# Inverse-times-value and score-times-f products of a delta-rule layer on four 64x64 TensorE tiles, with the second key head's f crossed between the partition halves

## The chip, the cores and the metric

The kernel runs on one core of a Trainium2 chip. The metric is the device time of one execution in microseconds, the median of several runs. Each core has a matrix engine (PE, TensorE; its weight loads are shown as PEld), a vector engine (DVE), a scalar engine (ACT), a general engine (POOL, GpSimd) and a queue engine that issues DMAs (SP). Each of them works through its own instructions in order and waits for the others by semaphores.

## The reference, cut to what matters

The program is two transformer layers on an input of 2 batches x 1024 tokens x 256. Layer 0 adds a gated delta-rule attention and a mixture of low-rank experts; layer 1 adds a gated linear attention and a sparsified feed-forward unit. The change lies in the delta-rule layer, which takes most of the time. It has 16 key heads of 128 and 32 value heads of 128; two value heads share a key head. After projections, a causal convolution over four tokens and SiLU, each value head runs this recurrence over its tokens:

```
S = S * exp(g_t)                      # state, 128 x 128
kv = k_t @ S
delta = (v_t - kv) * beta_t
S = S + outer(k_t, delta)
o_t = q_t @ S
```

with q and k normalized, g and beta from a second projection. The outputs are multiplied by SiLU(z), normalized by their root mean square, scaled, and projected by W_out.

## The kernel before

All is in float32, for which each matrix product is issued as two instructions.

**Tiling.** The 128 partitions hold both batches side by side: a chunk is 64 tokens of batch 0 in the lower half (LO) and the same 64 tokens of batch 1 in the upper half (HI). A head group is 4 value heads and their 2 key heads (8 groups); a unit is one group and 512 columns, that is 4 chunks (4 units to a group); a pair is two chunks. There are 64 pairs and 128 chunks. The recurrence is done chunk by chunk, with the inverse of a unit triangular 64x64 matrix for each head and batch.

**Steps of a pair.** `pair_scores` (L489) multiplies keys by keys and queries into the PSUM tile kq (PE, L520), and by the decays lb on DVE (L526) into np: np[:, 0] for the inverse, np[:, 1] for the outputs. SP then copies np[:, 0] in two ways: four DMAs into nat (L530), and two DMAs to DRAM (natd, L536), from where eight small DMAs (L540) gather n, the 8x8 diagonal blocks. `pair_lanes` inverts these on DVE in a chain of small operations on X (L558 to L582) and sends the result E through DRAM (ed, L584) into U (L586). `pair_inverse` joins blocks to 32 with two rounds of 32x32 products (L603), then to 64 (px L660, xs L663, pyt L669), and leaves the transposed inverses in invT, where they are copied by L654 and L671. invT is a 128x128 block diagonal for each head: batch 0's inverse at LO x LO, batch 1's at HI x HI, zeros elsewhere, set once.

**Steps of a chunk.** `chunk_tokens` (L675) turns keys and values to tokens by partitions: ktok on POOL (L688), vtok on ACT (L697). `chunk_state` multiplies the old state by keys (pks) and queries (pqs, both L716), subtracts pks from vtok on DVE (L719), scales the state on POOL (L724), forms pf = invT x vtok (L734), copies it to f on ACT (L736), multiplies keys with f into pS (L743) and scores with f into po (L747), adds pS to the state on DVE (L754), po to qs (L758), multiplies by z (L760), and squares on ACT (gsq, L765). `chunk_output` computes the root mean square on POOL (ms and rms, L775 to L779), scales z (L782), turns it (yT, L786, copied to yTs on ACT, L788) and projects it (out, L792); DVE adds that to the result (L794).

pf is four products over all 128 partitions, one for each head. pS works on 64x64 tiles: from each half of the partitions to both halves of a PSUM tile, one bank for each batch. po works on two 64x64 tiles only: LO to LO and HI to HI, in one bank.

**Order.** The loop over pairs of `delta_layer` (L835) has steps of several pairs in flight: the scores and lanes of pair p, the inverse of p - 1, states of p - 2, the last outputs of p - 3, and convolutions of later units. `in_windows` (L817) merges them by due times, and a scheduler places each engine's instructions; the order is fixed when the program is built. The first chunk of a pair is called even here, the second odd.

**Buffers.** PSUM has 8 banks in one rotating pool of 512-column tiles, all under one tag, for the whole program. Work tiles have two buffers unless another number is given.

```
add("scores", 0.0, 0.45, pair_scores(k, pools, pair(p)))
add("lanes", 0.65, 0.9, pair_lanes(k, pools, pair(p)), "scores")
add("inverse", 0.0, 1.0, pair_inverse(k, pools, pair(p - 1)))
add("tokens0", 0.5, 1.0, chunk_tokens(k, pools, pair(p - 1).chunks[0]), "state0")
add("tokens1", 0.0, 0.4, chunk_tokens(k, pools, two))
add("state0", 0.0, 0.5, chunk_state(k, pools, one))
add("state1", 0.5, 1.0, chunk_state(k, pools, two), "state0", "tokens1")
```

Of the kernel before, what the change touches and what calls it, by code (L numbers as in the profile page):

```python
# [9 lines left out]
F32 = mybir.dt.float32  # L10
# [4 lines left out]
P = 128  # L15
D = 256
KT = D // P
NB = 2
# [161 lines left out]
def delta_gates(k, pool, I):  # L180


    nc = k.nc
    shape = [P, NTILE, HV]
    wba = pool.tile([P, KT, 2 * HV], F32, tag="wba", name="wba")
    nc.sync.dma_start(wba, I["W_ba"].rearrange("(kt p) c -> p kt c", p=P))
    dtb = pool.tile([P, HV], F32, tag="dtb", name="dtb")
    nc.scalar.dma_start(dtb, I["dt_bias"].partition_broadcast(P))
    na = pool.tile([P, HV], F32, tag="na", name="na")
    nc.scalar.dma_start(na, I["A_log"].partition_broadcast(P))  # L190

    nbeta = k.gates.tile(shape, F32, tag="nbeta", name="nbeta")
    g = pool.tile(shape, F32, tag="g", name="g")
    x = pool.tile(shape, F32, tag="spx", name="spx")
    for t, rows in thin_projection(k, pool, "ba", wba, 2 * HV):
        pv = rows.rearrange("p t (m c) -> p t m c", m=HK)
        mine = lambda a: a[:, t : t + TPB, :].rearrange("p t (m c) -> p t m c", m=HK)
        nc.scalar.activation(mine(nbeta), pv[:, :, :, 0:2], AF.Sigmoid)
        nc.vector.tensor_copy(mine(x), pv[:, :, :, 2:4])
        yield  # L200
    nc.vector.tensor_scalar(nbeta, nbeta, -1.0, None, ALU.mult)
    yield
    nc.vector.tensor_tensor(x, x, bcast(dtb, 1, NTILE), ALU.add)
    yield

    u = pool.tile(shape, F32, tag="spu", name="spu")
    nc.scalar.activation(u, x, AF.Abs)
    nc.scalar.activation(u, u, AF.Exp, scale=-1.0)  # L210
    s = pool.tile(shape, F32, tag="sps", name="sps")
    nc.vector.tensor_scalar(s, u, 2.0, None, ALU.add)
    yield
    nc.vector.reciprocal(s, s)
    yield
    nc.vector.tensor_tensor(s, s, u, ALU.mult)
    yield
    s2 = pool.tile(shape, F32, tag="sps2", name="sps2")
    nc.vector.tensor_tensor(s2, s, s, ALU.mult)
    yield  # L220
    nc.vector.tensor_scalar(u, s2, 1.0 / 17.0, None, ALU.mult)
    yield
    for d in (15, 13, 11, 9, 7, 5, 3):
        nc.vector.scalar_tensor_tensor(u, u, 1.0 / d, s2, ALU.add, ALU.mult)
        yield
    nc.vector.scalar_tensor_tensor(u, u, 1.0, s, ALU.add, ALU.mult)
    yield
    nc.vector.tensor_scalar(x, x, 0.0, None, ALU.max)
    yield
    nc.vector.scalar_tensor_tensor(x, u, 2.0, x, ALU.mult, ALU.add)  # L230
    yield
    nc.scalar.activation(na, na, AF.Exp)
    nc.vector.tensor_scalar(na, na, -1.0, None, ALU.mult)
    yield
    nc.vector.tensor_tensor(g, x, bcast(na, 1, NTILE), ALU.mult)
    yield

    flat = lambda a: a.rearrange("p t h -> p (t h)")
    sums = {}
    for name, lhsT in (("neG", k.upto), ("nrev", k.after)):  # L240
        ps = ps_tile(k, f"sum_{name}")
        nc.tensor.matmul(ps, lhsT, flat(g), start=True, stop=True)
        sums[name] = k.gates.tile(shape, F32, tag=name, name=name)
        nc.scalar.activation(flat(sums[name]), ps, AF.Exp)
        yield
    k.eEnd = k.gates.tile([P, NB, NTILE, HV], F32, tag="eEnd", name="eEnd")
    for b, rows in enumerate((LO, HI)):
        ps = ps_tile(k, f"sum_end{b}")
        nc.tensor.matmul(ps, k.ones[rows], flat(g)[rows], start=True, stop=True)
        nc.scalar.activation(flat(k.eEnd[:, b]), ps, AF.Exp)  # L250
        yield
    for name in ("neG", "nrev"):
        nc.vector.tensor_scalar(sums[name], sums[name], -1.0, None, ALU.mult)


    gT = pool.tile([HV, NTILE, P], F32, tag="gT", name="gT")
    for t0 in range(0, NTILE, 4):
        ps = ps_tile(k, f"gT{t0}")
        for i in range(4):
            nc.tensor.transpose(ps[0:HV, i * P : (i + 1) * P], g[:, t0 + i, :], k.ident)  # L260
        nc.scalar.copy(gT[:, t0 : t0 + 4, :].rearrange("h t c -> h (t c)"), ps[0:HV, :])
        yield
    k.grows = k.dram.tile([NGROUP, NB, NTILE, HPG, CT], F32, tag="grows", name="grows")
    for b in range(NB):
        mine = gT[:, :, b * CT : (b + 1) * CT]
        nc.vector.memset(mine[:, :, 0:1], -1e30)
        for n in range(NGROUP):
            nc.sync.dma_start(k.grows[n, b].rearrange("t h c -> h t c"), mine[n * HPG : (n + 1) * HPG])
    k.nbeta = nbeta
    k.neG, k.nrev = sums["neG"], sums["nrev"]  # L270
# [218 lines left out]
def pair_scores(k, pools, pr):  # L489
# [6 lines left out]

    nc, wk, h = k.nc, pools.work, pr.h
    pr.nat = wk.tile([P, PC, HPG, B], F32, tag="nat32", name=f"nat32{pr.name}")  # L500
    pr.n8 = wk.tile([P, W, W], F32, tag="n8", name=f"n8{pr.name}")
# [19 lines left out]
    yield  # L521
    pr.np = pools.np.tile([P, 2, PC, HPG, CT], F32, tag="np", name=f"np{pr.name}")
    pairs = lambda a: a.rearrange("p x (m j) i -> p (x m) j i", m=KPG)
    for s in range(2):
        by = kq[:, :, :, s].rearrange("p x m i -> p (x m) i")
        nc.vector.tensor_tensor(pairs(pr.np[:, s]), pairs(lb), bcast(by, 2, 2), ALU.mult)  # L526
        if s == 0:
            yield
    for n, r in enumerate(QUARTERS):
        nc.sync.dma_start(pr.nat[r], pr.np[r, 0, :, :, QUARTERS[n % 2]])  # L530

# [78 lines left out]
def pair_inverse(k, pools, pr):  # L610
# [40 lines left out]
    invT = pr.invT.rearrange("p x h c -> p (x h) c")  # L651
    full = pr.np[:, 0].rearrange("p x h c -> p (x h) c")
    for n, r in enumerate(QUARTERS):
        (nc.gpsimd.tensor_copy, nc.scalar.copy)[n % 2](invT[r, :, r], U[r])  # L654
    yield
    px = part(k, f"px5_{pr.name}", B)
    for i in range(PH):
# [10 lines left out]
            lo, hi = QUARTERS[q], QUARTERS[q + 1]  # L668
            nc.tensor.matmul(pyt[lo, i, :], xs[hi, i, :], U[hi, i, :], start=True, stop=True)  # L669
    for q, copy in ((0, nc.scalar.copy), (2, nc.vector.tensor_copy)):  # L670
        copy(invT[QUARTERS[q], :, QUARTERS[q + 1]], pyt[QUARTERS[q]])  # L671
    yield


def chunk_tokens(k, pools, x):  # L675

    nc, wk, h, c = k.nc, pools.work, x.h, x.c
    if not x.last:
# [4 lines left out]
        kt = wk.tile([P, KPG, P], F32, tag="kt", name=f"kt{x.name}", bufs=1)  # L683
        nc.scalar.copy(kt, pk[:, 0:KPG, :])  # L684
        x.k = wk.tile([P, HPG, P], F32, tag="ktok", name=f"ktok{x.name}")
        pair = lambda a: a.rearrange("p (m i) c -> p m i c", m=KPG)
        wend = h.wend[:, c, :].rearrange("p (m i) -> p m i", m=KPG)
        nc.gpsimd.tensor_tensor(pair(x.k), bcast(kt, 2, 2), bcast(wend, 3, P), ALU.mult)  # L688
        yield
    pv = four(k, f"pv{x.name}")  # L690
    for i in range(HPG):
# [8 lines left out]

def chunk_state(k, pools, x):

    nc, wk, h, c = k.nc, pools.work, x.h, x.c
    t = h.t0 + c
    at = lambda a, i: a[:, t, h.h0 + i : h.h0 + i + 1]
# [3 lines left out]
    if not x.first:  # L709
        pks, pqs = four(k, f"pks{x.name}"), four(k, f"pqs{x.name}")  # L710
        for s, out in ((0, pks), (1, pqs)):
            for m in range(KPG):
                two = slice(2 * m, 2 * m + 2)
                for b, rows in halves:
                    q = of_chunk(h.kq[m][:, s], c, b)
                    nc.tensor.matmul(out[rows, two, :], q, k.S[:, b, two, :], start=True, stop=True)  # L716
        yield
        for i in range(HPG):
            nc.vector.scalar_tensor_tensor(  # L719
# [9 lines left out]
            nc.scalar.activation(qs[:, i, :], pqs[:, i, :], AF.Copy, scale=at(k.neG, i))  # L729
        yield  # L730

    pf = four(k, f"pf{x.name}")
    for i in range(HPG):
        nc.tensor.matmul(pf[:, i, :], invT[:, i, :], x.v[:, i, :], start=True, stop=True)  # L734
    f = wk.tile([P, HPG, P], F32, tag="f", name=f"f{x.name}")
    nc.scalar.copy(f, pf)  # L736
    yield
    if not x.last:
        pS = [four(k, f"pS{x.name}_{b}") for b in range(NB)]
        for i in range(HPG):  # L740
            for b, rows in halves:
                for cols in (LO, HI):
                    nc.tensor.matmul(pS[b][cols, i, :], x.k[rows, i, cols], f[rows, i, :], start=True, stop=True)  # L743
    po = four(k, f"po{x.name}")
    for i in range(HPG):
        for b, rows in halves:
            nc.tensor.matmul(po[rows, i, :], x.pair.np[rows, 1, x.at, i, :], f[rows, i, :], start=True, stop=True)  # L747
    yield
    if not x.last:
        for b in range(NB):  # L750
# [2 lines left out]
            else:  # L753
                nc.vector.tensor_tensor(k.S[:, b], k.S[:, b], pS[b], ALU.add)  # L754
    yield
    no = po
    if not x.first:
        nc.vector.tensor_tensor(qs, qs, po, ALU.add)  # L758
        no = qs
    nc.vector.tensor_tensor(x.z, no, x.z, ALU.mult)  # L760
    yield
    x.sumsq = pools.small.tile([P, HPG], F32, tag="sumsq", name=f"sumsq{x.name}")
    for i in range(HPG):
# [71 lines left out]
def delta_layer(k, I):  # L835
    nc, tc = k.nc, k.tc
    with ExitStack() as ctx:
# [9 lines left out]
        k.normw = const.tile([P, 1], F32, tag="normw", name="normw")  # L847
        nc.sync.dma_start(k.normw, I["norm_w"])
        k.tails = const.tile([P, 4 * KPG, NB, KSIZE - 1], F32, tag="tails", name="tails")
        k.invT = [const.tile([P, PC, HPG, P], F32, tag=f"invT{i}", name=f"invT{i}") for i in range(2)]  # L850

        k.S = const.tile([P, NB, HPG, P], F32, tag="S", name="S")
        k.X8 = [const.tile([P, W, W], F32, tag=f"X8{i}", name=f"X8{i}") for i in range(2)]
# [495 lines left out]
def two_layers(ctx, tc, I, out):  # L1349
# [1 line left out]
    k = Ctx()  # L1351
    k.nc, k.tc = nc, tc
    k.keep = ctx.enter_context(tc.tile_pool(name="keep", bufs=1))
    k.psum = ctx.enter_context(tc.tile_pool(name="psum", bufs=8, space=bass.MemoryType.PSUM))

    k.res = k.keep.tile([P, NTILE, D], F32, tag="res", name="res")
    k.mv = k.keep.tile([P, NTILE, 2], F32, tag="mv1", name="mv1")
# [5 lines left out]
    make_constants(k, k.keep)  # L1363
    k.xnT = k.keep.tile([P, KT, N], F32, tag="xnT", name="xnT")

    with tc.tile_pool(name="ln0", bufs=2) as pool:
        tiles = {}

# [9 lines left out]
    with ExitStack() as scope:  # L1378
        k.gates = scope.enter_context(tc.tile_pool(name="d_gates", bufs=1))
        k.dram = scope.enter_context(tc.tile_pool(name="d_dram", bufs=1, space=bass.MemoryType.DRAM))  # L1380
        expert_layer(k, I)
        delta_layer(k, I)

    with ExitStack() as scope:
        pool = lambda name, bufs: scope.enter_context(tc.tile_pool(name=name, bufs=bufs))
        pools = Pools()
        pools.const, pools.work, pools.h = pool("l1_const", 1), pool("l1_work", 2), pool("l1_h", 2)
        xn = pools.const.tile([P, NTILE, D], F32, tag="xn1", name="xn1")
# [67 lines left out]
```

## Time and profile before

| what | value |
|---|---|
| median of 3 runs | 2953.18 us (2949.0 to 2954.69) |
| profiled execution: time, span | 2948.61 us, 2946.9 us |
| delta layer in steady state | about 400 to 2550 us |
| PE busy there | 1970.56 of 2150 us |
| DVE, ACT, POOL busy there | 1489.82, 1402.51, 1354.81 us |
| pf on PE (L734) | 1024 instructions, 167.1 us busy |
| po on PE (L747) | 2048 instructions, 135.1 us busy |
| pS on PE (L743) | 3840 instructions, 132.5 us busy |
| ktok on POOL (L688) | 120 instructions of 1213 ns |
| DMAs on SP's queue for each pair | lb 2, nat 4, natd 2, n 8, ed 1, U 1 |

A row "A L1 <- B L2: x, n, m" of the waits says that engine A sat idle before its instruction of line L1 until engine B's of line L2 had ended, x us in total, n times, m us the longest. A row of the timeline gives the start, the duration, the engine, the line, what is written from what, shapes, and how many instructions are merged in the row; in brackets stand the idle time before it and what ended that. The durations of matrix instructions overlap at their ends, so the pitch of a series is read from start to next start. The name of a tile is that of the program, without its pair's number.

### The profile page before, as it was taken

How to read it: one execution, taken by the hardware profiler on the slowest of the kernel's cores; microseconds unless marked ns; L12 is line 12 of the kernel's file. 1: busy time of each engine (PE TensorE's matmuls, PEld its weight loads, DVE VectorE, ACT ScalarE, POOL GpSimd, SP SyncE). 2: the span in 40 equal slices, each digit the busy share in tenths (PEclk: the TensorE clock that was granted, in tenths of full speed). 3: DMA queues.
4: the chain of work that ended last, by engine and by line, in shares of the span. 5: the costliest groups of instructions: out<-in, count | busy, mean ns of one | idle time of the engine just before them, and what ended most of it. 6: DMA issues, size and time to landing. Idle time of an engine off the chain costs nothing.

```text
span 2946.9 us, 87779 instructions
## 1 busy us (share of the span) xinstructions
PE 2647.8 (90%) x36502; PEld 1680.6 (57%) x36502; DVE 1914.8 (65%) x3845; ACT 1716.6 (58%) x4121; POOL 1516.5 (51%) x2690
## 2 busy tenths in 40 slices
PE   6998689998999899989999999999989998989997
PEld 2444356665666566655655666566655665654565
DVE  7652666676677666767767666677676677645544
ACT  4432566675666666666666667666666666544321
POOL 2222456666666666666666666666665666630000
PEclk9998899999999999999999999999999999999999
DMA  3001111111111111111111111111111111110000
GB/s 77 4 1 57 37 28 35 36 43 28 35 35 43 28 35 35 44 28 43 34 38 28 42 35 35 28 42 36 36 27 35 28 37 20 29 57 3 1 15 15
DMA packets 265965, 95.22 MB, mean 32 GB/s; under 512 B 220512, under 2 KB 244192, under 8 KB 265568
## 3 DMA queue, kind: packets, MB, share of 16 engines
q1 hardware_dynamic: 261872, 86.67, 13.2%
q8 instruction: 287, 4.70, 0.7%
q10 hardware_dynamic: 3696, 2.95, 0.4%
q14 instruction: 110, 0.90, 0.1%
HBM read 53.63 MB, written 27.53 MB: 28 GB/s over the span
## 4 chain that ended last, share of the span: by engine, by line
PE 32%; DVE 22%; ACT 13%; POOL 12%; issue 7%; DMA 7%; SPq 6%; DVEq 0%; POOLq 0%; ACTq 0%
DVE conv L363 6%; PE pj L152 5%; SPq L540 3%; PE out L792 3%; ACT gsq L765 3%; DMA n<-natd 3%; DVE qs L758 2%; DMA natd<-np 2%; DVE S L754 2%; POOL S L724 2%; DVE z L760 2%; PE y L1074 2%; POOL rn L447 2%; PE pg L152 2%; SPq L530 2%
## 5 line engine op out<-in xcount | busy, mean ns | idle before, releaser
L363 DVE SCALAR_TENSOR_TENSOR conv<-raw,convw,conv 128x512 f32<-128x512 f32 x768 | 644.3, 841 | 188.6 <-ACT conv L358 184.2
L152 PE MATMUL pj<-xnT,w 128*128 128x512 f32 x1024 | 509.4, 622 | 8.5 <-DMA w<-in_W_qkvz 8.5
L792 PE MATMUL out<-wo,yTs 128*128 128x256 f32 x1024 | 284.1, 425 | 106.7 <-ACT yTs L788 106.7
L719 DVE SCALAR_TENSOR_TENSOR vtok<-pks,neG,vtok 128x128 f32<-128x128 f32 x480 | 144.8, 342 | 251.7 <-PE pks L716 247.4
L765 ACT ACTIVATE gsq<-z 128x128 f32<-128x128 f32 x512 | 157.7, 308 | 246.3 <-DVE z L760 240.9
L152 PEld LDWEIGHTS pj<-xnT,w 128*128 128x128 f32 x1024 | 188.8, 197 | 187.0 <-issue 182.1
L792 PEld LDWEIGHTS out<-wo,yTs 128*128 128x128 f32 x1024 | 200.6, 206 | 143.0 <-ACT yTs L788 113.4
L724 POOL TENSOR_TENSOR S<-S,eEnd 128x512 f32<-128x512 f32 x224 | 257.7, 1170 | 26.7 <-PE pqs L716 26.3
L152 PE MATMUL z<-wz,xnT 128*128 128x512 f32 x512 | 240.4, 593 | 0.0
L356 ACT COPY raw<-pj 128x512 f32<-128x512 f32 x256 | 147.5, 576 | 144.3 <-PE pj L152 95.5
L754 DVE TENSOR_TENSOR S<-S,pS 128x512 f32<-128x512 f32 x224 | 148.5, 684 | 123.8 <-POOL S L724 110.8
L734 PE MATMUL pf<-vtok,invT 128*128 128x128 f32 x1024 | 167.1, 289 | 31.4 <-DVE vtok L719 31.2
L347 POOL COPY raw<-tails 128x6 f32<-128x6 f32 x192 | 68.8, 359 | 239.4 <-DVE conv L363 189.7
L358 ACT ACTIVATE conv<-pj,convw 128x512 f32<-128x512 f32 x256 | 176.9, 691 | 0.0
L729 ACT ACTIVATE qs<-pqs,neG 128x128 f32<-128x128 f32 x480 | 136.3, 365 | 56.9 <-PE pqs L716 54.9
L372 ACT ACTIVATE kq<-conv 128x512 f32<-128x512 f32 x128 | 81.3, 635 | 144.3 <-DVE conv L363 141.4
L734 PEld LDWEIGHTS pf<-vtok,invT 128*128 128x128 f32 x1024 | 135.9, 190 | 50.8 <-DVE vtok L719 43.2
L782 POOL TENSOR_TENSOR z<-z,rms 128x512 f32<-128x512 f32 x128 | 145.5, 1136 | 10.1 <-POOL rms L779 0.2
L688 POOL TENSOR_TENSOR ktok<-kt,wend 128x512 f32<-128x512 f32 x120 | 145.6, 1213 | 7.5 <-ACT kt L684 7.5
L360 POOL COPY tails<-raw 128x6 f32<-128x6 f32 x192 | 60.7, 316 | 156.5 <-ACT raw L356 156.5
L743 PE MATMUL pS<-f,ktok 64*64 64x128 f32 x3840 | 132.5, 275 | 7.6 <-ACT f L736 7.5
L603 PE MATMUL px<-L,natm 32*32 32x32 f32 x8192 | 101.7, 198 | 40.8 <-DVE L L645 22.7
(323 smaller groups left out, 5885.0 us busy)
## 6 DMA issues: line engine op xcount, KB each, us to landing
lb<-grows SPq DMA_DIRECT2D x128, 128.0 KB
natd<-np SPq DMA_DIRECT2D x128, 128.0 KB
w<-in_W_qkvz SPq DMA_DIRECT2D x16, 512.0 KB
nat<-np SPq DMA_DIRECT2D x256, 32.0 KB
n<-natd SPq DMA_DIRECT2D x512, 4.0 KB
ed<-E SPq DMA_DIRECT2D x64, 128.0 KB
U<-ed SPq DMA_DIRECT2D x64, 128.0 KB
wz<-in_W_qkvz SPq DMA_DIRECT2D x16, 256.0 KB
```

Source lines behind the costliest of these rows:

```text
L152: k.nc.tensor.matmul(ps, lhsT_of(kt), rhs_of(kt), start=(kt == 0), stop=(kt == KT - 1))
L356: nc.scalar.copy(chunks(raw[:, :, KSIZE - 1 :]), pv)
L358: nc.scalar.activation(chunks(y), pv, AF.Copy, scale=tap(KSIZE - 1))
L363: k.anchor = nc.vector.scalar_tensor_tensor(y, shifted, tap(j), y, ALU.mult, ALU.add).ins
L688: nc.gpsimd.tensor_tensor(pair(x.k), bcast(kt, 2, 2), bcast(wend, 3, P), ALU.mult)
L719: nc.vector.scalar_tensor_tensor(x.v[:, i, :], pks[:, i, :], at(k.neG, i), x.v[:, i, :], ALU.mult, ALU.add)
L724: nc.gpsimd.tensor_tensor(k.S[:, b], k.S[:, b], bcast(k.eEnd[:, b, t, h.h0 : h.h0 + HPG], 2, P), ALU.mult)
L734: nc.tensor.matmul(pf[:, i, :], invT[:, i, :], x.v[:, i, :], start=True, stop=True)
L754: nc.vector.tensor_tensor(k.S[:, b], k.S[:, b], pS[b], ALU.add)
L765: nc.scalar.activation(sq, x.z[:, i, :], AF.Square, accum_out=x.sumsq[:, i : i + 1])
L782: nc.gpsimd.tensor_tensor(y, y, bcast(rms, 2, P), ALU.mult)
L792: nc.tensor.matmul(po[:, 0:D], yT[:, i, :], wo[:, i, :], start=(i == 0), stop=(i == HPG - 1))
```

## The change

- invT holds, for each head, only the two 64x64 blocks: batch 0's in LO, batch 1's in HI. The copies L654 and L671 write there.
- pf is made of eight products of 64x64 tiles instead of four of 128x128. For key head m = 0 they stay in their half (LO to LO, HI to HI), for m = 1 they cross (LO to HI, HI to LO). So f of the second key head's two value heads has batch 0 in HI and batch 1 in LO.
- po multiplies by this f, and crosses back for m = 1, so that the outputs stand as before. The score halves np[:, 1] of m = 1 must then be crossed: DVE writes them into a tile npo (one buffer), and two DMAs on SP's queue move its halves across.
- pS needs crossed keys for m = 1: POOL writes these into a tile ktoko, and two DMAs on SP's queue for each chunk move its halves into ktok. The state S and its decay eEnd have the batches of m = 1 exchanged.
- pf and po of a chunk share a PSUM tile fo of two banks, one bank for each key head, with one buffer. The other PSUM tiles of the delta layer rotate over 6 banks instead of 8. The layers before and after have pools of 8 of their own.

```diff
+        by_key = lambda a: a.rearrange("p (t g m j) -> p t g m j", t=NTILE, g=NGROUP, m=KPG)
+        for m in range(KPG):
+            mine = by_key(flat(k.eEnd[:, b ^ m]))[:, :, :, m]
+            nc.scalar.activation(mine, by_key(ps)[:, :, :, m], AF.Exp)
...
+    by = kq[:, :, :, 0].rearrange("p x m i -> p (x m) i")
+    nc.vector.tensor_tensor(pairs(pr.np[:, 0]), pairs(lb), bcast(by, 2, 2), ALU.mult)
+    yield
+    other = wk.tile([P, PC, 2, CT], F32, tag="npo", name=f"npo{pr.name}", bufs=1)
+    for m, out in enumerate((pr.np[:, 1, :, 0:2], other)):
+        two = slice(2 * m, 2 * m + 2)
+        nc.vector.tensor_tensor(out, lb[:, :, two], bcast(kq[:, :, m, 1], 2, 2), ALU.mult)
+    for rows, across in ((LO, HI), (HI, LO)):
+        nc.sync.dma_start(pr.np[across, 1, :, 2:4], other[rows])
     for n, r in enumerate(QUARTERS):
         nc.sync.dma_start(pr.nat[r], pr.np[r, 0, :, :, QUARTERS[n % 2]])
...
-        nc.gpsimd.tensor_tensor(pair(x.k), bcast(kt, 2, 2), bcast(wend, 3, P), ALU.mult)
+        other = wk.tile([P, 2, P], F32, tag="ktoko", name=f"ktoko{x.name}")
+        for m, out in ((1, other), (0, x.k[:, 0:2])):
+            wend = h.wend[:, c, 2 * m : 2 * m + 2]
+            nc.gpsimd.tensor_tensor(out, bcast(kt[:, m], 1, 2), bcast(wend, 2, P), ALU.mult)
+        for rows, across in ((LO, HI), (HI, LO)):
+            nc.sync.dma_start(x.k[across, 2:4], other[rows])
...
-    pf = four(k, f"pf{x.name}")
-    for i in range(HPG):
-        nc.tensor.matmul(pf[:, i, :], invT[:, i, :], x.v[:, i, :], start=True, stop=True)
+    fo = k.psum2.tile([P, KPG, 2, 2, P], F32, tag="fo", name=f"fo{x.name}")
+    pf, po = fo[:, :, 0], fo[:, :, 1]
+    across = lambda r, m: halves[r ^ m][1]
+    for i in range(2):
+        for m in range(KPG):
+            for r, rows in halves:
+                n = 2 * m + i
+                nc.tensor.matmul(pf[across(r, m), m, i, :], invT[rows, n, :], x.v[rows, n, :], start=True, stop=True)
...
-    po = four(k, f"po{x.name}")
-    for i in range(HPG):
-        for b, rows in halves:
-            nc.tensor.matmul(po[rows, i, :], x.pair.np[rows, 1, x.at, i, :], f[rows, i, :], start=True, stop=True)
+    for i in range(2):
+        for m in range(KPG):
+            for r, rows in halves:
+                n = 2 * m + i
+                nc.tensor.matmul(
+                    po[across(r, m), m, i, :], x.pair.np[rows, 1, x.at, n, :], f[rows, n, :], start=True, stop=True
+                )
...
+        early.close()
+        with psum("psum1", 6) as k.psum, psum("psum2", 1) as k.psum2:
+            delta_layer(k, I)
```

## The prediction

> **What bounds the kernel now.** I read the page first (shares, chain), then who waited for whom within 400 to 2550 us, where the delta layer is in steady state, then one pair of chunks in the timeline, engine by engine.
>
> The page's shares (busy us, share of the span, instructions), and its chain by engine:
>
> ```profile
> PE 2647.8 (90%) x36502; PEld 1680.6 (57%) x36502; DVE 1914.8 (65%) x3845; ACT 1716.6 (58%) x4121; POOL 1516.5 (51%) x2690
> ...
> PE 32%; DVE 22%; ACT 13%; POOL 12%; issue 7%; DMA 7%; SPq 6%; DVEq 0%; POOLq 0%; ACTq 0%
> ```
>
> The two disagree. PE is busy 90%, so a faster PE should pay nearly in full; but only a third of the chain that ended last lies on PE. The waits of the stage (us in total, times, longest), PE's and DVE's, decide between them:
>
> ```profile
> PE out L792 <- ACT yTs L788: 103.5, 51, 3.4
> PE pf L734 <- DVE vtok L719: 31.2, 47, 1.5
> PE pyt L669 <- DVE xs L663: 20.2, 14, 2.5
> ```
>
> ```profile
> DVE S L754 <- POOL S L724: 110.6, 90, 5.0
> ...
> DVE X L558 <- DMA n<-natd: 9.8, 18, 1.7
> ```
>
> PE's longest wait is for yTs. ACT is late with it because it first squares z (L765), z is behind S, S and qs on DVE, and DVE's S waits for POOL's scaling of S (L724), in 90 chunks. So I followed one pair round. DVE, POOL and SP (start, duration, and in brackets the idle time before and its releaser):
>
> ```profile
> 1616.91 0.69 DVE L760 TENSOR_TENSOR z<-qs,z 128x512 f32<-128x512 f32 x1
> ...
> 1628.80 0.69 DVE L754 TENSOR_TENSOR S<-S,pS 128x512 f32<-128x512 f32 x1 [0.31 <-POOL S L724]
> ...
> 1630.73 1.28 DVE L526 TENSOR_TENSOR np<-lb,kq 128x512 f32<-128x512 f32 x2
> ...
> 1644.93 0.28 DVE L558 COPY X<-n 128x4 f32<-128x4 f32 x1 [1.08 <-DMA n<-natd]
> ```
>
> ```profile
> 1620.26 0.20 POOL L775 TENSOR_TENSOR ms<-sumsq,q 128x4 f32<-128x4 f32 x1 [0.87 <-ACT gsq L765]
> ...
> 1626.29 2.48 POOL L724 TENSOR_TENSOR S<-S,eEnd 128x512 f32<-128x512 f32 x2
> ```
>
> ```profile
> 1596.00 2.66 SPq L530 DMA_DIRECT2D nat<-np  x4
> ...
> 1631.44 2.65 SPq L530 DMA_DIRECT2D nat<-np  x4
> 1634.13 1.25 SPq L536 DMA_DIRECT2D natd<-np  x2
> 1635.48 1.19 SPq L596 DMA_DIRECT2D lb<-grows  x2
> 1637.18 4.26 SPq L540 DMA_DIRECT2D n<-natd  x8
> ```
>
> A closed loop is to be seen, from nat (1596.00) to the next nat (1631.44), 35.44 us: nat to X, through natd, DRAM and n, 13.60 (X at 1609.60); X to the end of z on DVE, hardly idle, 8.00; z through ACT's squares to POOL's ms 2.66; POOL without a gap from ms to the end of S 8.51; S, qs, z and np on DVE to nat 2.67. No pf and no po lies on it. Asking what np waited for in all pairs: in six of every eight, POOL's S; in two (the first of a head group, which has no S to scale, and the next), PE's kq. PE runs beside the loop with some 3 us of waiting a pair.
>
> X has two paths of nearly one length. In 19 of 64 pairs DVE waits for n (12.3 us, 0.65 each); in the rest it comes later, from out over pj, pks and vtok, also without pf or po. From the end of the last n issue to X, the waiting pairs show 2.2 to 3.5 us and most of the others 1.9 to 3.5: n has little cover, by my estimate 0 to 1 us, 0.4 on average.
>
> **The change part by part.** The sum is made against the profiled execution, 2948.61 us (span 2946.9); the median, 2953.18, lies 4.6 above and I add the result to it.
>
> pf and po on four tiles. PE's order stays the same, so this is a matter of pitch:
>
> ```profile
> 1607.18 1.16 PE L734 MATMUL pf<-vtok,invT 128*128 128x128 f32 x8
> 1608.18 1.88 PE L152 MATMUL z<-wz,xnT 128*128 128x512 f32 x4
> ...
> 1612.14 1.10 PE L743 MATMUL pS<-f,ktok 64*64 64x128 f32 x32
> 1613.07 1.05 PE L747 MATMUL po<-f,np 64*64 64x128 f32 x16
> 1614.05 0.69 PE L660 MATMUL px<-L,np 32*32 32x32 f32 x32
> ```
>
> From start to the next start, pS puts 32 instructions on four tiles into 0.93 us, 29 ns each; po, on two tiles, 16 into 0.98 (61 ns); pf 8 into 1.00 here, 0.90 in other pairs (113 ns). On four tiles both become 16 x 29 ns = 0.46: pf saves 0.44, po 0.52, 0.96 a chunk, 123 us of PE over 128 chunks. The Trainium skill, TensorEngine Tiling (Array Packing), Restrictions and Gotchas, speaks against it: different row tiles cannot use one PSUM bank at once. In the new pf and po each bank takes both row halves (m = 0 straight, m = 1 crossed), while pS gives each row half a bank of its own. By the rule the pairs within a bank would serialize: two-way at best, 0.92 each, nothing saved. But the old po already writes from both row halves into one bank, at 61 ns against 4 x 29 = 116 for a tile alone: it overlaps. I go by the row. The same page's Key Properties say that a change of tiling mode drains the array; pf now differs from its 128x128 neighbours, one or two changes more a chunk. The nearest rows, the weight loads before pS and px, show 0.17 us of idle: up to 128 x 0.34 = 44 us of PE, which the waits beside the loop cover as well.
>
> What the saving is worth: on the loop, nothing in six pairs of eight. Before pyt (L669) PE now comes about 1 us sooner, but in 39 of 64 pairs it already waits for DVE's xs there or comes within 0.35 us of it, so the saving turns into that wait; in the even chunk it turns into the wait for yTs. In the 16 pairs where kq releases np, pf (and in half of them po) is ahead of kq: 16 x 0.44 + 8 x 0.52 = 11 us, of which I take 8, since pf also waits for vtok.
>
> SP, the scores' crossing. In the built order the first nat stays first, then come the two crossings of np, then the other nats and natd. An issue in a row costs 0.6 to 0.66 us (nat, natd, lb): 2 x 0.63 = 1.26. They wait for the third DVE product: np's second half, 0.64 us, becomes two of 128x256, nearest row 0.41 (L643, also with PSUM), ready 0.86 after the first; less the 0.66 of the first nat, 0.2. natd and n are 1.46 later. That is on the loop. Less the cover of 0.4, X is 1.05 later in some 60 pairs: +63 us. Bounds: cover of 1.0 gives +28; no cover and 0.2 more for the crossing's bytes ahead of natd's gives +100.
>
> Part comes back: where POOL's S runs beside DVE's small X operations, L564 takes 0.97 us instead of 0.16; in two pairs of eight X starts within it, and a later X meets less of it. 16 pairs x 0.6: -10; bounds 0 and -16.
>
> ktok's crossing. POOL's one product (1213 ns) becomes two of 128x256 (nearest, natm: 751 each, at best 0.55): 0 to 0.3 us more a chunk, behind S in POOL's order, so off the loop. Its DMAs stand in SP's queue just ahead of nat (odd chunk) and of ed (even). POOL's S ends 2.67 before nat; the half product 0.6 and two issues 1.26 make 1.9: it fits. In the first pair of each group POOL ends ktok after np (1517.5 against 1517.3), and nat waits about 1.1: 8 pairs, +9. What is queued behind is natd and the loop. Before pS the crossed ktok has over 10 us, the crossed np more than a whole pair; nothing for either.
>
> ACT. f now stands behind two invT copies (63 odd chunks, before: 2) or two vtok (45 chunks, before: 8): f is 0.8 us later. pS is 3 us behind f in the odd chunk (z, pj, pv between): covered. In the even chunk px (0.7) lies between; if that is too little, PE waits up to 0.5, beside the loop.
>
> PSUM, six rotating banks and fo. Following the order, each reuse six tiles on finds its reader done 1 us or more before (closest: out behind S, pj behind np). fo is read by qs and z 7 us before the next pf. No cost; if a cover fails, tenths on PE. The pool change at both ends, eEnd in four ACT instructions for two: +1.
>
> Sum: +63 - 8 - 10 + 9 + 1 = +55; 2953 + 55 = 3008 us.
>
> **The rivals.**
> PE is the bound after all (faster). For it: 90% busy, wait for pks 241.7 us on DVE. Its place is pf and po in each chunk; its price is -123 in full, about 2830, and with PE's waits as now half of it, about 2890. It decides if n lands 1.5 us or more before DVE asks for it. Against: POOL releases S in 90 chunks and 19 pairs already wait for n.
> Both sides hidden: n has a cover near 1.2 us, X moves 0.3 and the 16 pairs gain: +16 - 8 - 10 = about 2950; for it are the pairs with gaps of 3 us and more before X.
> SP becomes the bound: six more issues a pair, 11.4 + 3.8 us of 36.5, with waits for POOL ahead of nat and ed. Another 1 us in each pair, +60: 3068. Against: the order of the queue follows the order in time.
> Four tiles do not overlap: PE saves nothing and still runs beside the loop; +8 instead of -8: 3024.
>
> **How the numbers follow.** The forecast (with the case of no overlap) 0.64, the hidden case 0.18, PE 0.11, SP 0.07. The forecast's bounds give 2970 to 3045. The range 2930 to 3055 leaves out PE's case and most of SP's. What differs by less than 0.2% (6 us) this measurement can't tell from no change. Faster: PE 0.11, and half of the hidden case, 0.09; same: 0.05; slower: the rest, 0.75.
>
> **What would show it.** pf and po at 16 instructions in about 0.46 us each; PE busy down by some 120 us and its share to about 84%; the wait of DVE's X for n up from 12 us to 60 or more, in most pairs; nat to X at about 14.7 us; PE's wait for xs (L669 before) above 60 us; np still released by POOL's S. Wrong if X waits no more than now and the stage shortens, or if pf and po keep 0.9 us.

## The result, and the profile after

The changed kernel takes 3015.94 us (3011.22 to 3023.08, 4 runs) against 2951.09 (2947.78 to 2954.69, 4 runs) for the kernel before: a ratio of 1.0224, 95% interval 1.0202 to 1.0247. The forecast was 3008, within its range, and on the right side. The experiments below show that the forecast's reason was nevertheless wrong: the DMAs that it charged with 63 us cost about 7, and the shorter products, which it valued at nothing, cost about 60.

The page of the changed kernel, shares and the chain by engine:

```profile
PE 2644.9 (88%) x37526; PEld 1610.7 (53%) x37526; DVE 1882.0 (62%) x3909; ACT 1713.5 (57%) x4123; POOL 1524.2 (51%) x2810
...
PE 28%; DVE 26%; ACT 13%; POOL 12%; issue 9%; SPq 6%; DMA 6%; DVEq 0%; ACTq 0%; POOLq 0%
```

PE is busy as long as before (2647.8), in a span 66 us longer. The products did get shorter. The groups of pf (now L756), po (L772) and out (L819; before 284.1 us busy, 425 ns of one), busy time in us and mean ns behind the bar:

```profile
L756 PE MATMUL fo<-vtok,invT 64*64 64x128 f32 x2048 | 113.2, 288 | 16.6 <-DVE vtok L735 14.1
L772 PE MATMUL fo<-f,np 64*64 64x128 f32 x2048 | 80.2, 271 | 0.6 <-ACT f L760 0.5
L819 PE MATMUL out<-wo,yTs 128*128 128x256 f32 x1024 | 323.7, 470 | 162.3 <-ACT yTs L815 162.3
```

pf and po together went from 302.2 to 193.4 us: 109 saved. The same 1024 out products, which the change does not touch, take 40 us longer. The waits of the steady stage (400 to 2600 us), PE's and DVE's:

```profile
PE out L819 <- ACT yTs L815: 159.7, 51, 4.5
PE pyt L677 <- DVE xs L671: 23.2, 26, 3.9
```

```profile
DVE vtok L735 <- PE pks L732: 284.6, 106, 4.7
DVE S L781 <- POOL S L740: 135.9, 45, 7.0
DVE X L566 <- DMA n<-natd: 30.6, 20, 3.5
```

PE's wait for yTs grew from 103.5 us (in a stretch 50 us shorter) to 159.7 us in as many places: the saving on PE turned into that wait. And two lines speak against the forecast's account. X waits for n in 20 places, not in most pairs, and PE's wait for xs stayed. What then makes each pair longer? The mean granted clock of TensorE, 0.971 over the span before, is 0.944 after.

### The profile page after: what moved, and what is told of

It reads as the page before. It is cut to its first block, busy times and chain, and to the rows that moved or that the text cites. A ratio compares the mean times of both kernels' runs of the same rounds, so it can differ in the third digit from the quotient of the medians.

```text
span 3012.8 us, 90742 instructions
## 1 busy us (share of the span) xinstructions
PE 2644.9 (88%) x37526; PEld 1610.7 (53%) x37526; DVE 1882.0 (62%) x3909; ACT 1713.5 (57%) x4123; POOL 1524.2 (51%) x2810
## 4 chain that ended last, share of the span: by engine, by line
PE 28%; DVE 26%; ACT 13%; POOL 12%; issue 9%; SPq 6%; DMA 6%; DVEq 0%; ACTq 0%; POOLq 0%
DVE conv L366 7%; PE pj L152 4%; PE out L819 4%; DVE S L781 4%; ACT gsq L792 3%; SPq L548 3%; DVE qs L785 2%; POOL S L740 2%; DVE z L787 2%; DMA n<-natd 2%; DMA natd<-np 2%; PE y L1101 2%; PE pg L152 2%; PE base L152 2%; PE pd L1333 2%
## 5 line engine op out<-in xcount | busy, mean ns | idle before, releaser
L366 DVE SCALAR_TENSOR_TENSOR conv<-raw,convw,conv 128x512 f32<-128x512 f32 x768 | 637.5, 832 | 168.2 <-ACT conv L361 132.6
L152 PE MATMUL pj<-xnT,w 128*128 128x512 f32 x1024 | 525.6, 639 | 8.5 <-DMA w<-in_W_qkvz 8.5
L819 PE MATMUL out<-wo,yTs 128*128 128x256 f32 x1024 | 323.7, 470 | 162.3 <-ACT yTs L815 162.3
L819 PEld LDWEIGHTS out<-wo,yTs 128*128 128x128 f32 x1024 | 225.1, 231 | 207.7 <-ACT yTs L815 169.1
L735 DVE SCALAR_TENSOR_TENSOR vtok<-pks,neG,vtok 128x128 f32<-128x128 f32 x480 | 145.3, 343 | 302.2 <-PE pks L732 301.8
L450 POOL TENSOR_TENSOR rn<-sse,mhalf 128x16 f32<-128x16 f32 x32 | 98.9, 3089 | 116.2 <-DVE sse L463 113.3
L611 PE MATMUL px<-L,natm 32*32 32x32 f32 x8192 | 108.9, 205 | 50.3 <-DVE L L653 30.1
L363 POOL COPY tails<-raw 128x6 f32<-128x6 f32 x192 | 53.8, 280 | 185.0 <-ACT raw L359 184.4
L611 PEld LDWEIGHTS px<-L,natm 32*32 32x32 f32 x8192 | 93.7, 116 | 94.7 <-issue 83.0
L450 POOL TENSOR_TENSOR rms<-ms,mhalf 128x4 f32<-128x4 f32 x128 | 130.3, 1018 | 10.7
```

What stands on the lines that cost most here:

```text
L152: k.nc.tensor.matmul(ps, lhsT_of(kt), rhs_of(kt), start=(kt == 0), stop=(kt == KT - 1))
L366: k.anchor = nc.vector.scalar_tensor_tensor(y, shifted, tap(j), y, ALU.mult, ALU.add).ins
L450: nc.gpsimd.tensor_tensor(out, x, k.mhalf[:, 0 : x.shape[1]], ALU.pow)
L611: k.nc.tensor.matmul(out[r, i, :], lhsT[r, i, :], rhs[r, i, :], start=True, stop=True)
L735: nc.vector.scalar_tensor_tensor(x.v[:, i, :], pks[:, i, :], at(k.neG, i), x.v[:, i, :], ALU.mult, ALU.add)
L819: nc.tensor.matmul(po[:, 0:D], yT[:, i, :], wo[:, i, :], start=(i == 0), stop=(i == HPG - 1))
```

## Experiments

In each group the kernels ran with the kernel before on one chip, and the ratio is to that. Medians of different groups should not be compared directly: the kernel before alone gave 2955.4, 2957.1 and 2942.5 us.

### Without the crossing, and the crossing alone

e1 leaves out both crossings; e4 only that of the scores; e2 puts all six DMAs of a pair, and the split DVE and POOL products, into the kernel before, with spare DRAM as the DMAs' target; e3 moves the scores' two DMAs behind natd and n.

```diff
 # e1: np and ktok as before; all else as changed
-    for rows, across in ((LO, HI), (HI, LO)):
-        nc.sync.dma_start(pr.np[across, 1, :, 2:4], other[rows])
...
-        for rows, across in ((LO, HI), (HI, LO)):
-            nc.sync.dma_start(x.k[across, 2:4], other[rows])
 # e2: in the kernel before
+        nc.sync.dma_start(spare[across], pr.np[rows, 1, :, 2:4])
...
+            nc.sync.dma_start(spare[across], x.k[rows, 2:4])
 # e3: in the changed kernel
-    for rows, across in ((LO, HI), (HI, LO)):
-        nc.sync.dma_start(pr.np[across, 1, :, 2:4], other[rows])
...
         nc.sync.dma_start(pr.n8[at], src)
+    for rows, across in ((LO, HI), (HI, LO)):
+        nc.sync.dma_start(pr.np[across, 1, :, 2:4], other[rows])
```

Expected of e1:

> The changed kernel with nothing crossed: np and ktok are made as before the change, in one product each, and no crossing DMA is issued, so key head m = 1 multiplies values of the wrong batch (this part of the computation is changed). PE's instructions, fo, the six PSUM banks and eEnd stay as changed. Theory of the loop (nat, n, X, S, z, POOL, np): the 123 us that PE saves lie beside the loop, so 2926 to 2960 us against 2951 before. Rival, PE is the bound: about 2850. Rival, the loss comes from the PSUM pools or from PE's shorter products themselves: 2990 or more.

of e2:

> The kernel before, with the extra work of the crossing and nothing else: the second half of np in two DVE products, ktok in two POOL products, and the two plus four DMAs a pair at the same places in SP's program, but into spare DRAM tiles that nobody reads. PE unchanged. Theory of the loop: n comes 1.5 us later, the whole loss is here, 3000 to 3020 us. Rival, the loss comes from the four-tile products, PSUM or f's order on ACT: within 15 us of 2951.

of e3:

> The changed kernel with the two score-crossing DMAs behind natd instead of behind the first nat. Theory: natd and n are no longer late (n starts 6.7 us after np instead of 8.5), 2950 to 2975 us; what is left above the kernel with nothing crossed is the keys' crossing. Rival, the keys' DMAs or the waits of SP for POOL are what costs: still 3000 to 3016.

of e4:

> The changed kernel without the scores' crossing (np made as before, so the outputs of key head m = 1 take scores of the wrong batch), with the keys' crossing kept. Theory: 2945 to 2970 us, close to the one with the scores' crossing put late. Rival, the keys' DMAs in SP's queue ahead of nat and ed cost: 2990 or more.

Measured: e1 3013.72 us, ratio 1.0201 (1.0182 to 1.022); e4 3011.92, 1.0199 (1.0177 to 1.0221); e2 2963.57, 1.0024 (1.0012 to 1.0036); e3 2994.47, 1.0127 (1.0095 to 1.0159).

Taking the crossing away gives nothing back, and the crossing by itself costs 0.24%, some 7 us. (e2's DMAs go to DRAM and not across the partitions, and nothing waits for them; but the ratios of the changed kernel and of e1, 1.0224 and 1.0201, say the same of the real crossing.) The theory of the queue has fallen. In e2, DVE does wait for n:

```profile
DVE X L562 <- DMA n<-natd: 85.8, 47, 4.5
```

From 12.3 us in 19 places to 85.8 in 47, and X starts 1.28 us later after np than before, as late as in the changed kernel; yet a pair takes only 0.2 us more. A later X is not the loop's length. e3 is faster than the changed kernel, though not by what was expected, but the scheduler placed the instructions of DVE, POOL and ACT anew for it as well, so its gain is not a measure of those two DMAs; since e1, without them, gains less, I do not read it as one.

### The buffers, and the same program on two tiles

With the crossing out, the changed kernel still differs by its PSUM pools, by the place of f on ACT, and by the products themselves. p1 gives the kernel before the new pools alone. p4 is e1 with one thing different: each product goes to its own partition half, so that two tiles and not four work at once (the state and its decay follow). The orders of e1 and p4 are the same on PE, DVE, POOL and SP; on ACT only the set-up of eEnd differs.

```diff
 # p1: in the kernel before, and the three pools of the changed kernel
-    pf = four(k, f"pf{x.name}")
+    fo = k.psum2.tile([P, 2, HPG, P], F32, tag="fo", name=f"fo{x.name}")
+    pf, po = fo[:, 0], fo[:, 1]
 # p4: in e1
-    across = lambda r, m: halves[r ^ m][1]
+    across = lambda r, m: halves[r][1]
...
-                    nc.tensor.matmul(out[rows, two, :], q, k.S[:, b ^ m, two, :], start=True, stop=True)
+                    nc.tensor.matmul(out[rows, two, :], q, k.S[:, b, two, :], start=True, stop=True)
```

> The kernel before with the changed kernel's PSUM pools alone: six rotating banks, and one tile of two banks in a single buffer for the two products; products, layout and tiles as before. Buffer theory: near 3010 us, with the waits of the changed kernel. Clock theory: 2951 to 2960 us and a granted clock near 0.971. Order theory: 2951 us, unless ScalarE's order changes with the pools.

> The changed kernel's program (64-column inverses, 16 half products into one tile of two banks, six rotating banks), but with each product going from a partition half to the same half, and so nothing crossing: not four tiles at once but two. Clock theory, in which the shorter products do the harm: the products take about 0.5 us more per chunk, the waits for yTs get shorter, and the time falls to 2950 to 2980 us with a granted clock of 0.96 or more. Buffer and order theories: 3010 to 3030 us, as the kernel that only leaves out the crossing (3013.7 us).

Measured: p1 2947.75 us, 0.9971 (0.9956 to 0.9986), a little faster than the kernel before; p4 2957.19, 1.0001 (0.9987 to 1.0015).

So neither the pools nor f's place does harm: p4 has both and takes the time of the kernel before. From p4 to e1, with the order unchanged, nothing but faster products, and the ratio goes from 1.0001 to 1.0201. Making PE's work shorter is what costs the time. How, shows in PE's timeline of one pair at the same place of the program, first p4, then e1 (start, duration, engine, line, what, instructions):

```profile
1045.93 1.05 PE L762 MATMUL fo<-f,np 64*64 64x128 f32 x16
1046.91 1.09 PE L521 MATMUL kq<-kq 128*64 128x128 f32 x16
...
1049.76 0.60 PE L803 MATMUL yT<-ident,z 128*128 128x128 f32 x4
1050.29 0.75 PE L604 MATMUL pyt<-U,xs 32*32 32x32 f32 x64
1052.61 1.99 PE L809 MATMUL out<-wo,yTs 128*128 128x256 f32 x8 [1.57 <-ACT yTs L805]
1054.53 0.75 PE L604 MATMUL px<-L,natm 32*32 32x32 f32 x64
1055.21 1.98 PE L152 MATMUL pj<-xnT,w 128*128 128x512 f32 x4
1057.13 1.08 PE L722 MATMUL pks<-S,kq 128*64 128x256 f32 x8
```

```profile
1058.90 0.62 PE L765 MATMUL fo<-f,np 64*64 64x128 f32 x16
1059.45 1.09 PE L524 MATMUL kq<-kq 128*64 128x128 f32 x16
...
1062.30 0.60 PE L806 MATMUL yT<-ident,z 128*128 128x128 f32 x4
1062.83 0.75 PE L607 MATMUL pyt<-U,xs 32*32 32x32 f32 x64
1066.35 2.42 PE L812 MATMUL out<-wo,yTs 128*128 128x256 f32 x8 [2.77 <-ACT yTs L808]
1068.70 1.08 PE L607 MATMUL px<-L,natm 32*32 32x32 f32 x64
1069.71 2.70 PE L152 MATMUL pj<-xnT,w 128*128 128x512 f32 x4
1072.34 1.08 PE L725 MATMUL pks<-S,kq 128*64 128x256 f32 x8
```

po takes 0.55 us to the next start instead of 0.98. PE then reaches the odd chunk's out earlier, and waits 2.77 us for yTs instead of 1.57. And the same out, px and pj that follow take 5.99 us to the start of pks instead of 4.52. Nothing waits there; the products are slower. The granted clock by stretches says why, p4 and then e1 (from:to, length, PE busy, granted clock, DMA):

```profile
1050.36:1052.60 2.24, 0.68 (x64) 1.00 0.18 29
1052.60:1057.10 4.50, 4.49 (x76) 1.00 0.46 112
```

```profile
1062.90:1066.35 3.45, 0.68 (x64) 1.00 0.11 19
1066.35:1072.30 5.95, 5.95 (x76) 0.71 0.46 104
```

After the longer wait the clock is 0.71 over the stretch in which PE resumes, and 1.00 in p4. This stretch is on the loop: pks and pqs stand behind it, and POOL's scaling of S waits for pqs. POOL in p4 (out started at 1052.61) and in e1 (1066.35):

```profile
1059.15 2.69 POOL L730 TENSOR_TENSOR S<-S,eEnd 128x512 f32<-128x512 f32 x2 [0.20 <-PE pqs L722]
```

```profile
1074.36 2.48 POOL L733 TENSOR_TENSOR S<-S,eEnd 128x512 f32<-128x512 f32 x2 [1.70 <-PE pqs L725]
```

6.54 us after out, and 8.01: the 1.47 us are passed on whole. DVE's and POOL's work runs 1.2 to 1.3 us late through most of the pair that follows, and the yTs of the next odd chunk is 1.84 us late.

I cut each pair's period, from one odd out to the next, at the start of pks. "Resume" is from the start of out to pks, "rest" what follows; means over the same 52 steady pairs (us):

| kernel | period | resume | rest |
|---|---|---|---|
| before | 36.25 | 5.18 | 31.07 |
| p1, pools alone | 36.14 | 5.08 | 31.06 |
| p4, two tiles | 36.54 | 5.39 | 31.14 |
| e1, four tiles, no crossing | 37.46 | 6.29 | 31.18 |
| e4, keys' crossing | 37.39 | 6.28 | 31.11 |
| changed kernel | 37.33 | 6.20 | 31.12 |

The rest is 31.1 us in all of them, whether its products are short or long: shortening them buys nothing, as forecast. (In e2 it is 31.34, after a resume stretch of 5.14. In e3, whose order differs, it is 30.82 after one of 6.21: e3's gain lies in the rest.) All the difference is in the resume stretch. 1.02 us of it, times 62 such pairs in the run, is 63 us; the profiled spans differ by 65.9.

What decides the clock seems to be how long PE has had no large products. I counted from the end of yT to out, so that pyt's 32x32 products count as a gap, in those of the 52 pairs where only pyt lies between (38 in each kernel), over the twelve kernels here without spare products. Where the gap is under 3 us, the resume stretch runs at full speed (4.5 us) in 117 of 118 pairs; where it is over 4.5, in none of 71; between, in 88 of 267. Before, 20 of 38 such gaps are under 3 us, in p4 19, in the changed kernel and in e1 none. The Trainium skill, TensorE: Matmul & The Clock Gate, section "HAM oscillation — how this bites in real kernels", describes this: gaps of more than about 3.4 us drop the clock to half, and the next products start slow. The trace agrees in kind (half speed at worst: out takes 3.78 us instead of 1.99), but the length alone does not decide here: some gaps of 3.2 us were followed by a slow stretch, and some of 4.06 us were not.

The record of the granted clock in the traces settles what the length leaves open. It shows full and half speed and nothing between, and in each trace its changes lie within 6 ns of a fixed grid of steps of 3.413 us, whose place against the program's start differs from trace to trace. In e1, the odd outs at 542.48 and 843.83 us come after the same wait of 2.93 us. Three steps of the grid around each (from:to, length, PE busy, granted clock, DMA):

```profile
538.71:542.13 3.42, 0.85 (x66) 1.00 0.08 14
542.13:545.54 3.41, 3.06 (x7) 0.50 0.46 94
545.54:548.95 3.41, 3.41 (x74) 1.00 0.50 95
```

```profile
839.09:842.50 3.41, 1.81 (x70) 1.00 0.03 5
842.50:845.91 3.41, 2.08 (x26) 1.00 0.31 56
845.91:849.33 3.42, 3.42 (x78) 1.00 0.68 141
```

The first wait falls into one step: PE is busy for 0.85 of its 3.42 us, the whole next step is at half speed, and the resume stretch takes 6.01 us. The second wait is shared by two steps, neither is so empty, the clock stays, and the resume stretch takes 4.52 us. So it is over all. For each full-speed step between 400 and 2500 us, in all fourteen traces, I took the share of it that PE was busy with anything but 32x32 products. Half speed followed after all 308 steps with a share under 25%, after 6 of the 7302 with 50% or more, and after 89 of the 436 between. And of the 456 pairs counted above, the resume stretch runs at full speed in exactly the 205 in which no half-speed step lies in it; over all 456 its length fits 4.53 us and 0.45 us more for each us at half speed. So a longer gap does harm because it more often leaves a step of the grid nearly empty.

### Filling the wait

If the empty step does the harm, spare products in the gap should bring the time back. f1 and f2 issue four of them, 128x256, ahead of each odd chunk's out, in the changed kernel and in the kernel before.

```diff
     po = ps_tile(k, f"out{x.name}")
+    if x.at == 1:
+        for _ in range(4):
+            nc.tensor.matmul(po[:, D : 2 * D], k.ident, k.xnT[:, 0, 0:D], start=True, stop=True)
```

> The changed kernel with four spare 128x256 products, put into the unused half of the output tile, ahead of the output product of every second chunk, where TensorE stands idle 2.8 to 4.5 us for yTs; nothing else is changed. Clock theory: the products became shorter, so TensorE stands still longer there (idle ahead of the output product 162 us against 107 us before), its granted clock falls (0.944 against 0.971) and what comes after runs at half speed; with the gap filled the granted clock goes to 0.965 or more, the output products of the second chunks take 2.0 us for the pair of passes and not 3.4 to 3.8, and the time falls to 2930 to 2970 us. Buffer theory (six rotating banks and one double tile instead of eight) and order theory (f later on ScalarE): 1.9 us of more work per pair of chunks on TensorE gains nothing, 3016 us or up to 60 us more.

> The kernel before with the same four spare products at the same place. Clock theory: it too loses some of its time to a lower clock (0.971 over the run, 22 waits of over 2 us ahead of the output product), so the granted clock goes to 0.98 or more and the time falls to 2910 to 2945 us. Buffer and order theories: 2951 us, or more by the part of the 1.9 us per pair of chunks that the idle time does not hold.

Measured: f1 3040.49 us, 1.0277 (1.026 to 1.0294); f2 2961.49, 1.0011 (1.0 to 1.0023). Neither gains, f1 loses. The clock did what was expected, 0.964 and 0.983, and f1's row of out shows it:

```profile
L822 PE MATMUL out<-wo,yTs 128*128 128x256 f32 x1024 | 284.9, 427 | 66.6 <-ACT yTs L815 66.6
```

427 ns and 66.6 us of waiting instead of 470 and 162.3. The resume stretch fell to 4.72 us from 6.20, in f2 to 4.48 from 5.18. But the rest rose to 33.11 from 31.12, in f2 to 31.87 from 31.07. Two things lie in that: in the pairs without a wait the spare products cost their 1.9 us, and the scheduler counted them as work and made a new order, so that other waits took the place (f1, 400 to 2600 us):

```profile
PE pyt L677 <- DVE xs L671: 50.3, 30, 6.5
PE z L152 <- DVE S L781: 34.5, 22, 2.5
```

So the test is not clean: it shows that large products in the gap keep the clock up, not that the time comes back with it.

### Filling it with the order unchanged

The g kernels fill the gap without a change of order: the 32x32 products of pyt just ahead of the wait are issued tile by tile instead of four tiles in turn. The built order is otherwise the same on all engines. g2 is e1 with this, g1 the changed kernel, g3 the kernel before, g4 p1.

```diff
-        blocks32(k, pyt, xs, U)
+        if s == 3:
+            for r in QUARTERS:
+                for i in range(PH):
+                    nc.tensor.matmul(pyt[r, i, :], xs[r, i, :], U[r, i, :], start=True, stop=True)
+        else:
+            blocks32(k, pyt, xs, U)
```

> The changed kernel without any crossing (3013.7 us, clock 0.941), in which the 32 small products of the inverse's first step (pyt, the last work of TensorE ahead of the long wait for yTs in every second chunk) are issued tile by tile and no longer four tiles in turn, so that they follow each other on one tile: the same products, the same order of all else on every engine, 1 to 2.5 us more of TensorE time per pair of chunks (0.75 us now), in a place where TensorE then waits 3 to 4.6 us anyway. Clock theory: the wait gets shorter by as much, the output products behind it run at full clock (2.0 us and not 3.5 to 3.8), the granted clock rises from 0.941 to 0.96 or more, and the kernel gets FASTER by more work: 2955 to 2990 us. Any theory in which TensorE's work or another wait bounds: no change, or up to 130 us slower.

> The changed kernel itself with the same slower issue of the inverse's first step, order unchanged on all engines. Clock theory: faster than the changed kernel by 20 to 55 us, 2960 to 2995 us, granted clock 0.96 or more. Otherwise 3016 us or more.

> The kernel before with the same slower issue. Clock theory: it waits 2.0 us at that place on average and has fewer slow stretches (clock 0.971), so the gain is smaller: 2915 to 2945 us, granted clock 0.98 or more. Otherwise 2951 us or up to 100 us more.

> The kernel before with the changed kernel's PSUM pools (2947.8 us, the fastest so far), and the same slower issue: the candidate for a version that beats both. Clock theory: 2905 to 2940 us. Otherwise 2948 us or more.

Measured: g2 3000.05 us, ratio 1.0198 (1.018 to 1.0215); g1 3013.04, 1.0239 (1.0216 to 1.0262); g3 2947.57, 1.0016 (1.0004 to 1.0027); g4 2945.29, 1.0005 (0.9986 to 1.0023). By the ratios none gains, against the expectation. g2's timeline at the wait that ended e1's pair:

```profile
1091.22 0.60 PE L811 MATMUL yT<-ident,z 128*128 128x128 f32 x4
1091.75 1.91 PE L649 MATMUL pyt<-U,xs 32*32 32x32 f32 x64
1097.14 3.78 PE L817 MATMUL out<-wo,yTs 128*128 128x256 f32 x8 [3.48 <-ACT yTs L813]
```

pyt takes 1.91 us instead of 0.75, the wait is 3.48 instead of 4.63, and out still runs at half speed. In the 38 pairs of the gap counts, g2 waits 2.30 us on average, as p4 does (2.37), but its resume stretch is 6.12 us, near e1's 6.41 and not p4's 5.35. Small products, one 32x32 tile at a time, fill the wait but not the gap: counted from yT it is 4.14 us, e1's 4.20, p4's 3.05. A half-speed step lies in the resume stretch in 28 of the 38 pairs, in e1 in 34, in p4 in 18. So the clock follows more than whether PE is busy, and 32x32 products count for less in it: had I counted them in full in the shares above, half speed would have followed after 64 of 7663 steps with 50% or more, and not after 6 of 7302. Over the 52 pairs the resume stretch is 0.47 us shorter than e1's and the rest 0.22 longer. g2's traced period, 37.20 us, is thus 0.26 under e1's, which its ratio does not show; but the kernel before, too, was 12.9 us faster on that group's chip, 0.2 us a pair, so traces of the two groups can't be compared this finely.

The version that does best is p1, 0.29% under the kernel before; g4 adds nothing to it that could be measured.

## Why the prediction was right, and where it was wrong

The number was right, its cause was not. Step by step:

- **"pf and po on four tiles": right.** 16 instructions took 0.60 us (pf) and 0.55 (po) to the next start, 34 to 38 ns each, against the 29 taken. Products of two row halves into one bank overlap, as the old po's row said and the skill's rule on row tiles did not. The rows of the page give 109 us saved of 123.
- **"SP, the scores' crossing": this step failed.** The last n issue ends 1.67 us later (12.83 us after np's start, before 11.16), near the 1.46 forecast, and X starts 1.23 later, near 1.05 (nat to X: 14.39 on average, before 13.30). But X is later in e1 too (14.82 against 14.02), where n is as early as before: there it stands behind vtok, and so behind the slow resume stretch. In e2, with the crossing and no more slow stretches than before, X is 1.28 later and the period only 0.2. So the +63 was mis-sized nine times over, because a later X was charged whole to the loop: X's chain does not set the end.
- **"What the saving is worth: nothing": this step failed as well, and it is where the loss lies.** The mechanism up to the wait was right, the saving does turn into a wait. What was missed is that an emptier wait costs PE its speed afterwards, and that the stretch afterwards, through pks and pqs to POOL's S, is on the loop. Its size, 1.02 us times 62 pairs, happens to be the 63 us that the crossing was charged with: the number came out by luck.
- **"No pf and no po lies on it": right; but the loop drawn was not complete.** It starts X at natd and n. The other path that the text names, "out over pj, pks and vtok", also feeds POOL's S, and that branch was left out.
- **ACT and PSUM, no cost: right** (p4 1.0001, p1 0.9971). The gain of 10 us from DVE beside POOL, the 9 us of ktok ahead of nat and the 8 us of the kq pairs were not tested one by one.
- **The signs named:** PE's busy time should have fallen by 120 us and fell by 3, since slower products took back what pf and po had saved; its share is 88%, not 84%. X's wait for n rose to 30.6 us in 20 places, not over 60 in most pairs. PE's wait for xs is 23.2, not over 60. np stands behind POOL's S as before.
- **The rivals:** "Both sides hidden" was right about the crossing; with the clock unchanged it would have been near the result, as p4 is. "PE is the bound" fell with p4 against e1.

Shown: shorter products alone, with the order unchanged, make the kernel 2% slower; nearly the whole difference lies in the stretch after the wait; and that stretch is long where a half-speed step of the clock lies in it, and not otherwise. Such a step follows every step that PE left nearly empty and hardly any that it filled by half; between, the counts don't tell which. Open: by how much less 32x32 products count, and why; and a kernel that keeps the short products, keeps the order and keeps the clock, which would show the time coming back. Fillers of large products that the scheduler does not count were not tried.

## What to carry to other kernels

An engine off the critical path that is made faster only waits longer, and on TensorE a longer wait can cost speed afterwards: before a product is shortened, read how long PE waits after it, what follows the wait, and whether that lies on the loop. Where the same untouched instructions show a longer mean duration after a change, look at the granted clock by stretches, cut where it changes, before looking for a new wait. And to tell "later" from "longer", cut the period of a loop at one event and compare the two parts over all pairs; a start that moves with the sum proves nothing about which path moved it.

## What the hardware showed that was not expected

- The granted clock changed only on a grid of 3.413 us. A step of it in which PE was under 25% busy with anything but 32x32 products was followed by a step at half speed in 308 of 308 cases, one with 50% or more in 6 of 7302. Two waits of 2.93 us in one trace came out differently, by their place on the grid.
- 64 products of 32x32 issued tile by tile, over 1.91 us instead of 0.75, left 28 of 38 resume stretches with a half-speed step (34 with the quicker issue). Eight instructions of 128x256 over 1.99 us brought the mean resume stretch to 4.72 us, 4.5 being full speed.
- Four 64x64 tiles in turn, with products of both row halves going into each of two banks, ran at 34 to 38 ns an instruction, against 61 for two tiles.
